# Four columns a chunk copied by TensorE through PSUM, in a graph layer's gather

## The chip, the cores and the metric

The kernel runs on one core of a Trainium2 chip. The metric is the time of one execution in device microseconds; the time before is the median of three runs. PE is TensorE, DVE is VectorE, ACT is ScalarE, POOL is GpSimd and SP is the engine that here issues most DMAs.

## The reference

One message-passing layer on a graph with 12,500 nodes of 48 numbers and 400,000 edges that are sorted by their target:

```python
h = jnp.maximum(_layernorm(x, axis=-1), 0.0)
x_i, x_j = h[dst], h[src]
tmp = jnp.concatenate([x_i, x_j, edge_attr], axis=1)   # 48 + 48 + 32
hid = jax.nn.relu(tmp @ W1 + b1)                       # 128 wide
out = jax.ops.segment_sum(hid @ W2 + b2, dst, num_segments=12500)
return x + out
```

All numbers are float32.

## The kernel before

`tmp @ W1` is split into three parts. A first stage (`node_tables`) makes two tables over the nodes, `tab_a` for the target's part with the bias and `tab_b` for the source's part, each with 128 numbers a node, in DRAM. Of `tab_b` it also keeps a copy in SBUF, turned round: `bt` has the 128 numbers on the partitions and the nodes along the free dimension.

The second stage (`windows`) goes over the edges in 391 chunks of 1024, each of 8 tiles of 128 edges. Targets are sorted, so a chunk's targets lie in a window of at most 80 nodes, and their part comes by a product: `prepare` has DVE compare the targets with the window's numbers (`lhs`, L437), and `before` multiplies that with the window's rows of `tab_a` and the edges' 32 numbers into the PSUM tile `pre` (L459). The sources are random. Their part is added to `pre` in `gathered` (L480), and a tile of 128 edges gets it in one of three ways:

- by a **gather** on POOL (L429): an indirect DMA fetches 128 rows of `tab_b` into `gb`, and a product with the identity adds them;
- by **columns** (L379): for each edge one instruction on DVE or ACT copies a column of `bt`, at an address from a register, into a column of a tile `gt`; a transposing product adds it. DVE fills 226 such tiles in the run and ACT 252;
- by **rows** (L335): SP issues a small DMA for each edge, 16 a chunk, into `gs`; 96 tiles.

Then `hidden` (L497, DVE) applies the relu and writes `hid`; `compare` (L448, DVE) makes the matrix `hot` that says to which node of the window each edge goes, from the numbers 0 to 79 in the PSUM tile `wnum`; `fold` (L507, L510) multiplies both into `p_g`, and `add` (L522, DVE) adds that to a running segment in SBUF. W2 is applied to whole segments.

The order is written out by hand in the loop at the end of `windows`, and each engine runs its own instructions in that order. In iteration c, PE does `before` and `gathered` of chunk c-1 and `fold` of chunk c-2. DVE does L437 of chunk c, columns (28), L497 of chunk c-2, columns (28), L448 of chunk c-1, columns (11), L522 of chunk c-3, columns (8). ACT does little but its 84 columns. The columns' numbers lie in `cols`, with `STRIP` numbers a chunk; `parts_of` cuts them into parts, and before each part the engine loads the part's numbers into registers (L318). `taken_by(c)` is the chunk that uses a tile which is filled in iteration c, 6 later and less toward the end. `STOP` is the iteration from which no more columns are copied. The tiles `gt` come from 13 buffers in turn, `gb` from 8 and 3, `pre` and `p_g` from two each.

Of the kernel before, what the change touches and what calls it, by code (L numbers as in the profile page):

```python
# [8 lines left out]
F32 = mybir.dt.float32  # L9
# [7 lines left out]
P = 128  # L17
N, D, DE, HID, E = 12500, 48, 32, 128, 400000
# [7 lines left out]
W = 80  # L26
# [29 lines left out]
END = NT // T  # L56


STRIP = 160
PLACE = 67  # L60
FEWER = 372
STOP = END - 3


def parts_of(c):

    dve = ((0, 20), (20, 8), (28, 20), (48, 8), (56, PLACE - 56), (68, 8))
    act = tuple((76 + 12 * k, 8 if k == 6 and c % 8 == 7 else 12) for k in range(7))
    return [(True, *of) for of in dve] + [(False, *of) for of in act]


def taken_by(c):

    lead = LEAD - max(0, c - FEWER + 1) * (LEAD - END + STOP) // (STOP - FEWER)
    return c + lead
# [3 lines left out]
BASE = 2 * RPART  # L79

BT0 = 16512
SEG0 = 144352
SEG_SIZE = 8 * L


# [9 lines left out]
def tiles_of(first, part):  # L95

    n = (END - 1 - first) * part // P
    return [first + (P * (j + 1) + part - 1) // part for j in range(n)]


AT = {}
COLS_OF = {}
for dve in (True, False):
    AT[dve] = [0]
    for c in range(STOP):
        AT[dve].append(AT[dve][-1] + sum(n for of, _, n in parts_of(c) if of == dve))
        for j in range(AT[dve][-2] // P, AT[dve][-1] // P):
            COLS_OF.setdefault(taken_by(c), []).append((dve, j))
BYROWS = tiles_of(ROWS0, RPART)
EPS = 1e-5  # L110

# [156 lines left out]
def windows(nc, tc, gp, bt, ident, idx, raw, rhss, x_t, tab_a, tab_b, dst, edge_t, w2s, b2s,  # L268
# [5 lines left out]
    with ExitStack() as es:  # L274
# [10 lines left out]
        gtc = es.enter_context(tc.tile_pool(name="gtc", bufs=GTS))  # L285
# [6 lines left out]
        ps_w = es.enter_context(tc.tile_pool(name="ps_w", bufs=1, space=PSUM))  # L292


        wnum = ps_w.tile([P, W], F32, name="wnum")
        nc.vector.tensor_copy(wnum, wrow)


        bt8 = bt.bitcast(U8)
# [3 lines left out]
        gts = {}  # L303
# [23 lines left out]
        def rows(c, nodes):  # L327

            for k, n in enumerate(nodes):
                e = (c - ROWS0) * RPART + k  # L330
                of = BYROWS[e // P]
                if of not in gss:
                    gss[of] = gtp.tile([P, HID], F32, name="gs")
                n = n.with_bounds(min_val=0, max_val=4 * HID * (N - 1))
                nc.sync.dma_start(  # L335
                    gss[of].bitcast(U8)[e % P : e % P + 1, :],
                    tab8[bass.ds(n, 4 * HID)].rearrange("(o h) -> o h", o=1),
                )
# [15 lines left out]
        def columns(c, part):  # L354

            parts = parts_of(c)
            dve, at, n = parts[part]
            place = PLACE if at < PLACE <= at + n and c >= LAG else None
            end = AT[dve][STOP] // P * P
            first = AT[dve][c] + sum(n for of, _, n in parts[:part] if of == dve) if c < STOP else end  # L360
            n = max(0, min(n, end - first))
            engine = mybir.EngineType.DVE if dve else mybir.EngineType.Activation
            copy = nc.vector.tensor_copy if dve else nc.scalar.copy
            size = -(-n // 4) * 4 if place is None else place + 1 - at
            if not n:
                if place is not None:
                    st[c - LAG]["base"], = numbers(c, place, 1, engine, cols)
                return
            got = numbers(c, at, size, engine, cols)
            if place is not None:  # L370
                st[c - LAG]["base"] = got[place - at]
            for k, to in enumerate(got[:n]):
                j, e = divmod(first + k, P)
                if (dve, j) not in gts:
                    gts[dve, j] = gtc.tile([HID, P], F32, name="gt")
                to = to.with_bounds(
                    min_val=BT0, max_val=BT0 + 4 * (NPAD - 1), guaranteed_mod_val=0, out_of_modulus=4
                ) - BT0
                copy(gts[dve, j][:, e : e + 1], bt8[:, bass.ds(to, 4)].bitcast(F32))  # L379

        def span(c):

            return next(w for w, last in SPANS if c < last)
# [59 lines left out]
        def compare(c):  # L443

            n, w = st[c]["n"], span(c)
            hot = wh.tile([P, T * W], F32, name="hot")
            hot = hot[:, : T * w].rearrange("p (t w) -> p t w", w=w)
            nc.vector.tensor_tensor(  # L448
                hot[:, :n, :], wnum[:, :w].unsqueeze(1).to_broadcast([P, n, w]),
                rel[:, c * T : c * T + n].unsqueeze(2).to_broadcast([P, n, w]), op=ALU.is_equal,  # L450
            )
            st[c]["hot"] = hot

        def before(c):

            s = st[c]
            pre = ps_p.tile([P, T, HID], F32, name="pre")
            for t in range(s["n"]):
                nc.tensor.matmul(  # L459
                    pre[:, t, :], s["lhs"][:K, t * P : (t + 1) * P], s["rhs"][:K, :],  # L460
                    start=t % BANK == 0, stop=False, skip_group_check=True,
                )
            s["pre"] = pre
# [49 lines left out]
        def add(c):  # L513

            s, w = st.pop(c), span(c)
            k = group(c)[0] % 2
            of = SEG0 + k * SEG_SIZE
            at = s["base"].with_bounds(
# [44 lines left out]
        def ending():  # L563
# [36 lines left out]
        with tc.manual_schedule():  # L600
            for c in range(NCH):
                a = c - LAG
                g, k = group(a)
                if c < RAW:
                    raw_turn(c)
                if c == 0:
                    columns(c, 0)
                    columns(c, 1)
                if c < NCH:
                    prepare(c)  # L610
                    rows(c, st[c].pop("rows"))
                if 0 <= c - 1 < NCH:
                    before(c - 1)
                    gathered(c - 1)
                if c:
                    columns(c, 0)
                    columns(c, 1)
                columns(c, 6)
                columns(c, 7)
                if 0 <= c - 2 < NCH:  # L620
                    hidden(c - 2)
                    fold(c - 2)
                columns(c, 2)
                columns(c, 3)
                columns(c, 8)
                columns(c, 9)
                if 0 <= c - 1 < NCH:
                    compare(c - 1)
                segment_add()
                columns(c, 4)  # L630
                if a >= 0:
                    add(a)
                    if a + 1 == begin(g + 1) < NCH:
                        segment_next(g)
                columns(c, 5)
                columns(c, 10)
                columns(c, 11)
                columns(c, 12)
                if c < 2:
                    nc.vector.memset(segs[c], 0.0)  # L640
                if a + 3 == begin(g + 1) < NCH or c == NCH - 1:
                    segment_load(g)
                if g > 0 and k < L // BLK:
                    segment_sum(g - 1, k, BLK)
                if g > 0 and k == (STORE if begin(g + 1) < NCH else 2):
                    segment_store(g - 1, L)
                if c == 1:
# [132 lines left out]
def tile_gnn_preln(  # L780
# [284 lines left out]
```

## Time and profile before

| | |
|---|---|
| median of 3 runs | 5453.94 us (5451.19 to 5468.6) |
| the profiled execution | 5457.1 us |
| its span, first to last instruction | 5455.4 us |
| mean granted TensorE clock | 0.688 |
| gathers on POOL (L429) | 2551, 944 ns each |
| bytes moved by DMA | 304.34 MB, mean 56 GB/s |

A profile is one execution. A row of a group reads: line, engine, operation, tile written and tile read, shape, count; then busy time and the mean in ns of one; then the time that the engine stood idle just ahead of such instructions, and what ended most of it. "Issue" means that nothing the profile shows ended the wait. A row of the list of waits reads: engine, tile and line, what it waited for, and then us in total, times, and the longest. A row of the timeline reads: start and length in us, engine, line, operation and count, with the idle time ahead of it in brackets. A row of windows reads: the stretch, its length, busy time with the number of instructions in parentheses, granted clock, DMA share, GB/s. Instructions that load registers or only wait are not counted as busy.

### The profile page before, as it was taken

How to read it: one execution, taken by the hardware profiler on the slowest of the kernel's cores; microseconds unless marked ns; L12 is line 12 of the kernel's file. 1: busy time of each engine (PE TensorE's matmuls, PEld its weight loads, DVE VectorE, ACT ScalarE, POOL GpSimd, SP SyncE). 2: the span in 40 equal slices, each digit the busy share in tenths (PEclk: the TensorE clock that was granted, in tenths of full speed). 3: DMA queues.
4: the chain of work that ended last, by engine and by line, in shares of the span. 5: the costliest groups of instructions: out<-in, count | busy, mean ns of one | idle time of the engine just before them, and what ended most of it. 6: DMA issues, size and time to landing. Idle time of an engine off the chain costs nothing.

```text
span 5455.4 us, 119545 instructions
## 1 busy us (share of the span) xinstructions
PE 3461.6 (63%) x15545; PEld 2861.3 (52%) x15545; DVE 3429.6 (63%) x31063; ACT 3389.1 (62%) x32359; POOL 2455.9 (45%) x2615
## 2 busy tenths in 40 slices
PE   4476666666566666666665656767565666665657
PEld 3365555555555555555555545555454555554546
DVE  4466666666666666666666666666666666666666
ACT  3366666666666666666666666666666665666664
POOL 4344444444444444444444444444444444444441
PEclk7566666666676666666677676666766666777678
DMA  3211111111111111111111111122211121222221
GB/s 123 89 49 46 48 47 48 47 47 49 50 52 48 51 51 52 51 52 51 54 56 53 56 52 54 56 57 56 58 56 56 56 58 54 59 63 61 62 61 42
DMA packets 148917, 304.34 MB, mean 56 GB/s; under 512 B 61811, under 2 KB 87685, under 8 KB 140325
## 3 DMA queue, kind: packets, MB, share of 16 engines
q0 software_dynamic: 83168, 168.53, 11.0%
q1 hardware_dynamic: 64530, 127.90, 7.8%
q14 instruction: 685, 5.61, 0.3%
q8 instruction: 130, 2.13, 0.2%
q10 hardware_dynamic: 404, 0.17, 0.0%
HBM read 280.57 MB, written 18.39 MB: 55 GB/s over the span
## 4 chain that ended last, share of the span: by engine, by line
DVE 57%; issue 33%; DVEq 4%; PE 3%; another core or an unknown queue 2%; DMA 0%; ACT 0%; SPq 0%; POOL 0%; ACTq 0%
DVE gt L379 36%; DVE lhs L437 8%; DVE hid L497 8%; DVEq L318 4%; DVE hot L448 3%; DVE seg L522 1%; PE p_g L507 1%; PE pre L459 1%; PE p_n L212 1%; PE pre L480 0%; DVE xseg L557 0%; DVE seg L538 0%; DMA gs<-tab_b 0%; ACT tab L221 0%
## 5 line engine op out<-in xcount | busy, mean ns | idle before, releaser
L379 ACT COPY gt<-bt 128x1 f32 x32256 | 3337.6, 187 | 1850.0 <-issue 1802.1
L429 POOL DMA_INDIRECT gb<-tab_b,srci x2551 | 2408.4, 944 | 2882.9 <-PE pre L480 1899.2
L379 DVE COPY gt<-bt 128x1 f32 x28928 | 2183.2, 145 | 1729.8 <-issue 1672.5
L507 PE MATMUL p_g<-hot,hid 128*128 128x64 f32 (+4 forms) x6250 | 1173.5, 356 | 1838.2 <-remote 878.3
L507 PEld LDWEIGHTS p_g<-hot,hid 128*128 128x128 f32 x6250 | 1127.3, 278 | 2038.8 <-remote 927.3
L459 PE MATMUL pre<-rhs,lhs 112*128 112x128 f32 x6250 | 1283.0, 388 | 1.4 <-DVE lhs L437 1.4
L459 PEld LDWEIGHTS pre<-rhs,lhs 112*128 112x128 f32 x6250 | 1188.8, 292 | 59.2 <-issue 36.3
L480 PE MATMUL pre<-gb,ident 128*128 128x512 f32 (+3 forms) x1540 | 752.3, 618 | 0.0
L497 DVE TENSOR_SCALAR hid<-pre 128x1024 f32<-128x1024 f32 x391 | 475.0, 1215 | 44.1 <-issue 33.8
L437 DVE TENSOR_SCALAR_CACHE_REDUCE lhs<-row,bw 64x1024 f32<-64x1024 int16 (+4 forms) x391 | 492.3, 1259 | 8.1 <-issue 6.8
L480 PEld LDWEIGHTS pre<-gb,ident 128*128 128x128 f32 x1540 | 342.9, 248 | 254.8 <-issue 252.8
L448 DVE TENSOR_TENSOR hot<-wnum,rel 128x512 f32<-128x512 f32 (+4 forms) x391 | 208.1, 532 | 76.5 <-issue 74.3
L480 PE MATMUL pre<-ident,gt 128*128 128x128 f32 x478 | 141.8, 355 | 0.0
L510 PE MATMUL p_g<-ident,deg 64*128 64x64 f32 (+4 forms) x391 | 119.0, 304 | 0.0
L522 DVE TENSOR_TENSOR seg<-seg,p_g 128x128 f32 (+4 forms) x390 | 93.7, 240 | 14.8 <-issue 9.9
L480 PEld LDWEIGHTS pre<-ident,gt 128*128 128x128 f32 x478 | 89.9, 195 | 0.0
L510 PEld LDWEIGHTS p_g<-ident,deg 64*128 64x128 f32 (+4 forms) x391 | 69.7, 178 | 23.7
L221 ACT COPY tab<-p_n 128x512 f32<-128x512 f32 (+1 forms) x37 | 18.8, 526 | 99.1 <-remote 71.8
L212 PE MATMUL p_n<-wa,ht 97*128 97x256 f32 x98 | 33.2, 497 | 51.9 <-DVE tab L219 30.8
L212 PE MATMUL p_n<-wb,ht 96*128 96x256 f32 x98 | 29.2, 452 | 42.8 <-ACT tab L221 35.8
L212 PEld LDWEIGHTS p_n<-wa,ht 97*128 97x128 f32 x98 | 22.6, 243 | 61.9 <-DVE tab L219 33.4
L219 DVE COPY tab<-p_n 128x512 f32<-128x512 f32 x17 | 11.5, 687 | 65.2 <-remote 40.9
(90 smaller groups left out, 462.2 us busy)
## 6 DMA issues: line engine op xcount, KB each, us to landing
gs<-tab_b SPq DMA_DIRECT2D x6144, 0.5 KB
lhs<-in_edge_t SPq DMA_DIRECT2D x195, 256.0 KB
gb<-tab_b,srci POOLq DMA_INDIRECT x2551
row<-in_dst SPq DMA_DIRECT2D x45, 256.0 KB
row<-in_dst SPq DMA_DIRECT2D x43, 192.0 KB
row<-in_dst SPq DMA_DIRECT2D x25, 320.0 KB
row<-in_dst SPq DMA_DIRECT2D x43, 128.0 KB
tab_b<-tab SPq DMA_DIRECT2D x4, 1152.0 KB
```

Of the source, the lines that this page charges most:

```text
L212: nc.tensor.matmul(p_n[:, q, :], ht[:rows, r0 // 2 + g + q, :], wt.rearrange("k a h -> k (a h)"), start=True, stop=True,)
L318: return nc.values_load_multi_w_load_instructions(table[c % P : c % P + 1, c // P, at : at + n], engines=[engine], min_val=0, max_val=1 << 23,
L379: copy(gts[dve, j][:, e : e + 1], bt8[:, bass.ds(to, 4)].bitcast(F32))
L429: nc.gpsimd.indirect_dma_start(out=gb[:, t, :], out_offset=None, in_=tab_b[:, :], in_offset=bass.IndirectOffsetOnAxis(ap=srci[:, c * T + t ...
L437: nc.vector.tensor_scalar(lhs[:w, : n * P], row[:w, : n * P], bw[:w, c : c + 1], None, op0=ALU.is_equal, op1=ALU.add, accum_out=deg[:w, :1],)
L448: nc.vector.tensor_tensor(hot[:, :n, :], wnum[:, :w].unsqueeze(1).to_broadcast([P, n, w]), rel[:, c * T : c * T + n].unsqueeze(2).to_broad ...
L459: nc.tensor.matmul(pre[:, t, :], s["lhs"][:K, t * P : (t + 1) * P], s["rhs"][:K, :], start=t % BANK == 0, stop=False, skip_group_check=True,)
L480: nc.tensor.matmul(pre[:, t:e, :].rearrange("p t h -> p (t h)"), lhsT, rhs, start=False, stop=True, is_transpose=turned, skip_group_check= ...
L497: nc.vector.tensor_scalar(h[:, :n, :], s["pre"][:, :n, :], 0.0, None, op0=ALU.max)
L507: nc.tensor.matmul(p_g[:, 0, :], s["h"][:, t, :], s["hot"][:, t, :], start=t == 0, stop=t == n - 1)
L510: nc.tensor.transpose(p_g[:, 1, :], s["deg"][:w, :], ident[:w, :w])
L522: nc.vector.tensor_add(to, to, s["p_g"])
```

## The change

A third engine copies columns. `parts_of` gets a 14th part of four columns for PE, so a chunk has 164 numbers in place of 160. For each of the four, PE multiplies the identity with the column of `bt`, which puts the column into a PSUM tile of 128 columns, one of two (`turned_of`). When 128 are there, after 32 iterations, `held_tile` has DVE copy the tile to a `gt` in SBUF, from where it is used like the others. No bank of PSUM was free for that: `wnum`, which DVE reads in L448, and `turned_of` are now parts of one tile, `held`, of one bank. `STOP` goes from 387 to 386.

```diff
-STRIP = 160
+STRIP = 164
-STOP = END - 3
+STOP = END - 4
...
+    pe = ((160, STRIP - 160),)
+    return [(by, *of) for by, all_of in ((DVE, dve), (ACT, act), (PE, pe)) for of in all_of]
...
-        wnum = ps_w.tile([P, W], F32, name="wnum")
+        held = ps_w.tile([P, 4, P], F32, name="held")
+        wnum, turned_of = held[:, 0, :W], held[:, 1:3, :]
...
+                of = bt8[:, bass.ds(to, 4)].bitcast(F32)
+                if by == PE:
+                    nc.tensor.matmul(
+                        turned_of[:, j % 2, e : e + 1], ident, of, start=True, stop=True,
+                        skip_group_check=True,
+                    )
+                    continue
...
+        def held_tile(c):
+
+            for j in range(AT[PE][c] // P, AT[PE][c + 1] // P) if 0 <= c < STOP else ():
+                gts[PE, j] = gtc.tile([HID, P], F32, name="gt")
+                nc.vector.tensor_copy(gts[PE, j], turned_of[:, j % 2, :])
...
                     rows(c, st[c].pop("rows"))
+                columns(c, 13)
                 if 0 <= c - 1 < NCH:
                     before(c - 1)
                     gathered(c - 1)
...
                     compare(c - 1)
+                held_tile(c - 1)
                 segment_add()
```

On PE, early in the second stage, one iteration stood like this before (`p_g` is written by the fold of chunk c-2, `pre` by `before` and `gathered` of the chunk after the next):

```order
L510 MATMUL p_g<-ident,deg_97 128x16
L459 MATMUL pre<-rhs_87,lhs_859 128x128 [waits DMAHW6_49,PE_49]
L459 MATMUL pre<-rhs_87,lhs_859 128x128 x7
L480 MATMUL pre<-ident,gt 128x128
L480 MATMUL pre<-gs,ident 128x128 [waits DMAHW4_49,DMAHW3_49,DMAHW5_49,DMAHW2_49,DMAHW7_49,DMAHW1_49,DMAHW0_49]
L480 MATMUL pre<-gb,ident 128x512 [waits DMASW2_49,DMASW7_49,DMASW1_49,DMASW0_49]
L480 MATMUL pre<-gb,ident 128x256 [waits DMASW4_49,DMASW3_49]
L507 MATMUL p_g<-hot,hid 128x16 [waits DVE_49]
```

And the same place now, where the lines are some 20 higher (L530 was L510, L479 was L459, L500 was L480, L527 was L507):

```order
L530 MATMUL p_g<-ident,deg_97 128x16
L323 TENSOR_LOAD cols
L385 MATMUL held<-bt,ident 128x1 [waits DVE_49]
L385 MATMUL held<-bt,ident 128x1 x3
L479 MATMUL pre<-rhs_87,lhs_859 128x128 [waits DMAHW6_49,PE_49]
L479 MATMUL pre<-rhs_87,lhs_859 128x128 x7
L500 MATMUL pre<-ident,gt 128x128
L500 MATMUL pre<-gb,ident 128x512 [waits DMASW2_49,DMASW7_49,DMASW1_49,DMASW0_49]
L500 MATMUL pre<-gb,ident 128x384 [waits DMASW5_49,DMASW4_49,DMASW3_49]
L527 MATMUL p_g<-hot,hid 128x16 [waits DVE_49]
```

Between the fold of one chunk and L479 there are now a load of registers and four products, and the first product waits for DVE: for the L468 (was L448) of the iteration before, which reads the same tile `held`.

On DVE, one piece of an iteration before, from the compare to the next chunk's L437 (`seg` is the running segment):

```order
L448 TENSOR_TENSOR hot<-wnum,rel 128x256 [waits PE_49]
L318 TENSOR_LOAD cols
L379 COPY gt<-bt 128x1 x11
L522 TENSOR_TENSOR seg_850<-seg_850,p_g 128x2x32 [waits DVE_49,PE_49]
L318 TENSOR_LOAD cols
L379 COPY gt<-bt 128x1 x8
L437 TENSOR_SCALAR lhs_858,deg_95<-row,bw 32x1024 [waits DMAHW4_49]
```

And now:

```order
L468 TENSOR_TENSOR hot<-held,rel 128x256 [waits PE_49]
L323 TENSOR_LOAD cols
L393 COPY gt<-bt 128x1 x11
L542 TENSOR_TENSOR seg_850<-seg_850,p_g 128x2x32 [waits DVE_49]
L323 TENSOR_LOAD cols
L393 COPY gt<-bt 128x1 x8
L457 TENSOR_SCALAR lhs_859,deg_101<-row,bw 32x1024
```

The copies are the same. The compare now waits for the products of its own iteration, which stand behind the fold on PE, and so the add that follows no longer needs a wait for that fold: it waits for DVE alone.

More of the change, by code (lines that the diff above doesn't have):

```diff
@@ L56 @@
 END = NT // T
-STRIP = 160
+STRIP = 164
 PLACE = 67
 FEWER = 372
-STOP = END - 3
+STOP = END - 4
+DVE, ACT, PE = "DVE", "ACT", "PE"
 def parts_of(c):
@@ L68, in parts_of @@
     act = tuple((76 + 12 * k, 8 if k == 6 and c % 8 == 7 else 12) for k in range(7))
-    return [(True, *of) for of in dve] + [(False, *of) for of in act]
+    pe = ((160, STRIP - 160),)
+    return [(by, *of) for by, all_of in ((DVE, dve), (ACT, act), (PE, pe)) for of in all_of]
 def taken_by(c):
@@ L81 @@
 BT0 = 16512
-SEG0 = 144352
+SEG0 = 144416
 SEG_SIZE = 8 * L
@@ L102 @@
 COLS_OF = {}
-for dve in (True, False):
-    AT[dve] = [0]
+for by in (DVE, ACT, PE):
+    AT[by] = [0]
     for c in range(STOP):
-        AT[dve].append(AT[dve][-1] + sum(n for of, _, n in parts_of(c) if of == dve))
-        for j in range(AT[dve][-2] // P, AT[dve][-1] // P):
-            COLS_OF.setdefault(taken_by(c), []).append((dve, j))
+        AT[by].append(AT[by][-1] + sum(n for of, _, n in parts_of(c) if of == by))
+        for j in range(AT[by][-2] // P, AT[by][-1] // P):
+            COLS_OF.setdefault(taken_by(c), []).append((by, j))
 BYROWS = tiles_of(ROWS0, RPART)
@@ L356, in columns @@
             parts = parts_of(c)
-            dve, at, n = parts[part]
+            by, at, n = parts[part]
             place = PLACE if at < PLACE <= at + n and c >= LAG else None
-            end = AT[dve][STOP] // P * P
-            first = AT[dve][c] + sum(n for of, _, n in parts[:part] if of == dve) if c < STOP else end
+            end = AT[by][STOP] // P * P
+            first = AT[by][c] + sum(n for of, _, n in parts[:part] if of == by) if c < STOP else end
             n = max(0, min(n, end - first))
-            engine = mybir.EngineType.DVE if dve else mybir.EngineType.Activation
-            copy = nc.vector.tensor_copy if dve else nc.scalar.copy
+            engine = {
+                DVE: mybir.EngineType.DVE, ACT: mybir.EngineType.Activation, PE: mybir.EngineType.PE
+            }[by]
             size = -(-n // 4) * 4 if place is None else place + 1 - at
@@ L373, in columns @@
                 j, e = divmod(first + k, P)
-                if (dve, j) not in gts:
-                    gts[dve, j] = gtc.tile([HID, P], F32, name="gt")
                 to = to.with_bounds(
@@ L378, in columns @@
                 ) - BT0
-                copy(gts[dve, j][:, e : e + 1], bt8[:, bass.ds(to, 4)].bitcast(F32))
+                of = bt8[:, bass.ds(to, 4)].bitcast(F32)
[5 more added lines that the diff above has]
+                    continue
+                if (by, j) not in gts:
+                    gts[by, j] = gtc.tile([HID, P], F32, name="gt")
+                copy = nc.vector.tensor_copy if by == DVE else nc.scalar.copy
+                copy(gts[by, j][:, e : e + 1], of)
+        def held_tile(c):
+            for j in range(AT[PE][c] // P, AT[PE][c + 1] // P) if 0 <= c < STOP else ():
+                gts[PE, j] = gtc.tile([HID, P], F32, name="gt")
+                nc.vector.tensor_copy(gts[PE, j], turned_of[:, j % 2, :])
         def span(c):
@@ L1010 @@
     strip = np.zeros((SLOTS * P, STRIP), np.int32)
-    for dve in (True, False):
+    for by in (DVE, ACT, PE):
         tiles = {
             j: c * T + T - len(js) + k
-            for c, js in COLS_OF.items() for k, (of, j) in enumerate(js) if of == dve
+            for c, js in COLS_OF.items() for k, (of, j) in enumerate(js) if of == by
         }
@@ L1018 @@
         for c in range(STOP):
-            slot = [at + k for of, at, n in parts_of(c) if of == dve for k in range(n)]
-            strip[c, slot] = nodes[AT[dve][c] : AT[dve][c + 1]]
+            slot = [at + k for of, at, n in parts_of(c) if of == by for k in range(n)]
+            strip[c, slot] = nodes[AT[by][c] : AT[by][c + 1]]
     strip[LAG : NCH + LAG, PLACE] = first
```

## The prediction

> **What bounds the kernel now.** I read the page first: busy shares, then the chain of waits that ended last.
>
> ```profile
> PE 3461.6 (63%) x15545; PEld 2861.3 (52%) x15545; DVE 3429.6 (63%) x31063; ACT 3389.1 (62%) x32359; POOL 2455.9 (45%) x2615
> ...
> DVE 57%; issue 33%; DVEq 4%; PE 3%; another core or an unknown queue 2%; DMA 0%; ACT 0%; SPq 0%; POOL 0%; ACTq 0%
> ```
>
> No engine is busy two thirds of the time, yet the chain is DVE's almost alone: 57% in its instructions, 33% in "issue" (it stands still and the profile shows nothing it waits for), 4% in its queue. So the second view is what the engines wait for, with the groups of the column copies and of L507 ahead of it.
>
> ```profile
> L379 ACT COPY gt<-bt 128x1 f32 x32256 | 3337.6, 187 | 1850.0 <-issue 1802.1
> ...
> L379 DVE COPY gt<-bt 128x1 f32 x28928 | 2183.2, 145 | 1729.8 <-issue 1672.5
> L507 PE MATMUL p_g<-hot,hid 128*128 128x64 f32 (+4 forms) x6250 | 1173.5, 356 | 1838.2 <-remote 878.3
> ...
> POOL gb L429 <- PE pre L480: 1899.2, 271, 64.4
> ACT gt L379 <- issue: 1802.1, 2898, 1.9
> DVE gt L379 <- issue: 1672.5, 2806, 1.9
> ...
> DVE hid L497 <- PE pre L480: 10.2, 5, 4.3
> ```
>
> DVE waits 10.2 us for PE's largest result in the whole run, so PE does not hold it up. PE idles 1838.2 us ahead of L507, which is 4.7 us in each of 391 iterations: that is PE's slack. POOL is not short either, since it waits 1899.2 us for PE to give buffers back. What remains is DVE's own 75 copies an iteration and the "issue" time in which ACT stands still as well, for nearly as long (1802.1 and 1672.5 us).
>
> That time belongs to the gathers. The third view, windows over one source line, counts iterations (L437 shows two instructions in each) and then gathers (L429):
>
> ```profile
> 1000.00:5000.00 4000.00, 372.47 (x588) 0.69 0.19 54
> 5360.20:5395.50 35.30, 5.10 (x8) 0.89 0.15 43
> 5265.70:5283.00 17.30, 1.28 (x2) 0.70 0.22 57
> ...
> 1000.00:5000.00 4000.00, 1842.04 (x1951) 0.69 0.19 54
> 5360.20:5395.50 35.30, 0.00 (x0) 0.89 0.15 43
> 5265.70:5283.00 17.30, 10.15 (x11) 0.70 0.22 57
> ```
>
> From 1000 to 5000 us, 294 iterations take 13.61 us each with 6.64 gathers each. Four iterations without a gather take 8.83 us each. One with 11 gathers takes 17.3. So an iteration is about 8.8 us of DVE's own work plus 0.72 us a gather (4.78 / 6.64), or 0.77 by the single one (8.47 / 11), though no buffer of that gather is waited for.
>
> **The change, part by part.** The sum is made against the profiled execution, 5457.1 us; the median of the three runs, 5453.94, is 3.2 us below it.
>
> *Eleven gathers fewer.* PE fills 12 tiles (1544 columns / 128) and ACT one less (251 for 252); DVE keeps 226. That leaves 2540 gathers for 2551. At 0.72 to 0.77 us each that is 7.9 to 8.5 us; the lower end is 0.66 (1672.5 / 2551), or 7.3. I take **-8 us**. A later start of POOL's bursts costs nothing: it has 1899.2 us of waiting in hand.
>
> *Columns end sooner.* DVE's last 53 copies (28928 - 75 x 385) fall into iteration 385 before and after, so nothing is saved there. ACT ends in iteration 384 for 386. These rows show the end:
>
> ```profile
> 5390.70 2.33 ACT L379 COPY gt<-bt 128x1 f32 x24 [0.18 <-issue]
> ...
> 5396.85 0.28 DVE L379 COPY gt<-bt 128x1 f32 x3
> ```
>
> ACT's last copies end at 5393.03 while DVE is still copying, so ACT's 128 copies fewer are worth **0**. If ACT set the pace they would be worth 20.6 us ((3337.6 + 1850.0) / 32256 x 128).
>
> *DVE's add has one wait less.* The order shows L522 with waits for DVE and PE before, and for DVE alone after. The second wait takes an instruction of its own in DVE's queue, one that only waits; in the two built programs these are 681 and 323 on DVE, 358 fewer. The profile does not count them, so their price is bounded by what stands around L522 in an iteration without gathers:
>
> ```profile
> 5361.65 1.89 DVE L379 COPY gt<-bt 128x1 f32 x28
> 5363.46 1.21 DVE L497 TENSOR_SCALAR hid<-pre 128x1024 f32<-128x1024 f32 x1
> 5364.74 1.89 DVE L379 COPY gt<-bt 128x1 f32 x28
> 5366.55 0.81 DVE L448 TENSOR_TENSOR hot<-wnum,rel 128x640 f32<-128x640 f32 x1
> 5367.30 0.76 DVE L379 COPY gt<-bt 128x1 f32 x11
> 5367.98 0.31 DVE L522 TENSOR_TENSOR seg<-seg,p_g 128x160 f32 x1
> 5368.43 0.58 DVE L379 COPY gt<-bt 128x1 f32 x8
> ...
> 5372.42 1.22 DVE L497 TENSOR_SCALAR hid<-pre 128x1024 f32<-128x1024 f32 x1
> ...
> 5375.53 0.81 DVE L448 TENSOR_TENSOR hot<-wnum,rel 128x640 f32<-128x640 f32 x1
> ```
>
> L522 ends at 5368.29 and the next copy starts at 5368.43: 0.14 us in which DVE computes nothing and only its queue (the wait, L522, the load of the next eight numbers) can be at work. So the wait costs between 0, if the load hides it, and 0.14 us. The nearest row is the copies' own cadence, 0.06 us an instruction (11 in 0.76, the last one 0.15 long). I take a little under that, 0.048 us: 358 x 0.048 = **-17 us**; the ends are 0 and -50. This is the largest term, and the change does not mean it.
>
> *Twelve copies from PSUM on DVE.* Nearest row: the add of one 128x128 tile out of PSUM.
>
> ```profile
> L522 DVE TENSOR_TENSOR seg<-seg,p_g 128x128 f32 x90 | 25.0, 277 | 0.6 <-issue 0.6
> ```
>
> 12 x 0.277 is 3.3 us; a copy's cadence alone, 0.06, gives 0.7. I take **+3 us**. The wait for PE in front of it is for products of the iteration before.
>
> *PE's load and four products.* L507 issues two matmuls for one of the source (6250 for 3125), so four products are eight pairs. Their pace is read from L507 fast and slow:
>
> ```profile
> 5272.26 3.70 PE L507 MATMUL p_g<-hot,hid 128*128 128x80 f32 x16 [6.63 <-DVE hid L497]
> ...
> 5289.55 3.70 PE L507 MATMUL p_g<-hot,hid 128*128 128x80 f32 x16 [8.43 <-DVE hid L497]
> ...
> 5361.96 1.88 PE L480 MATMUL pre<-gb,ident 128*128 128x512 f32 x4
> 5364.73 2.01 PE L507 MATMUL p_g<-hot,hid 128*128 128x80 f32 x16 [0.89 <-DVE hid L497]
> 5366.57 0.23 PE L510 MATMUL p_g<-ident,deg 80*128 80x80 f32 x1
> 5366.65 1.99 PE L459 MATMUL pre<-rhs,lhs 112*128 112x128 f32 x16
> 5368.47 0.38 PE L480 MATMUL pre<-ident,gt 128*128 128x128 f32 x2
> 5368.69 1.45 PE L480 MATMUL pre<-gb,ident 128*128 128x512 f32 x4
> 5373.69 2.65 PE L507 MATMUL p_g<-hot,hid 128*128 128x80 f32 x16 [3.54 <-DVE hid L497]
> ```
>
> Eight pairs are 1.0 us at the pace of 2.01 for 16, and 1.85 at that of 3.70. The load of four numbers stands behind L507's work and should pass under it; if not, it adds some tenths. The first product also waits for DVE's L448 of the iteration before, since both use the tile `held`. Behind it stand L459 and L480, and for these waits DVE's L497 an iteration later; POOL and SP wait for them too, with the slack named above. In the rows: L448 ends at 5367.36, 0.6 us after PE's fold; with 1.0 us of products L459 starts near 5368.4 for 5366.65, and L480 ends near 5371.9 for 5370.14. PE's next L507 starts at 5373.69, so 1.8 us of its 3.54 us gap stay. DVE has more cover still: the L480 that ends at 5363.84 is read by the L497 of 5372.42, 8.6 us later, and L448 comes back after 9.0 us. Where PE idles only 0.89 us it falls behind by about a microsecond and catches up next time. I put down **+4 us** for the tightest places; the ends are 0 and the rivals below.
>
> *Weighing one rule.* After 8.43 us of idling L507 ran at 3.70 us, after 0.89 at 2.01. The Trainium skill, "TensorE: Matmul & The Clock Gate", section "HAM oscillation — how this bites in real kernels", says that a gap of over about 3.4 us puts the array back to half its clock; the trace agrees here, 8.43 against 0.89. The rule speaks against the change, since the new wait cuts PE's work in two and makes a second gap. By it PE would need the slow pace more often, which is the third rival.
>
> Sum: -8 - 17 + 3 + 4 = -18; 5457.1 - 18 = 5439, and by the 3.2 us between profile and median, **5436 us**.
>
> **Rivals.**
> 1. *The second wait was hidden.* If the load of the next numbers starts no sooner, -17 goes: -8 + 3 + 4 = -1, about 5453. For it: the queue runs ahead of the engine. Against it: 0.14 us without work at that place. Chance 0.25.
> 2. *PE becomes the bound, slower than before.* Place: the load and four products at register-given addresses, behind L507. ACT's and DVE's copies, which have such addresses too, stood still 0.62 and 0.60 us at a time while gathers ran (1802.1 / 2898, 1672.5 / 2806). Eight matmuls held like that cost 4.8 us, with the 0.8 of a load like it 5.6. It decides above 4.7 us an iteration, PE's slack: 0.9 us over, 385 times, is +350 us, near 5790. Below that it bites only in runs without gathers, like the four iterations from 5360.2: PE's slow pass (3.70 for L507, as much for L459, 1.9 for L480, about 9 us as they overlap) with 3.7 us of products exceeds 8.8 by 3.9. Three such runs give 12 x 3.9 = 47 less a cover of 8.6 in each, +21 on the forecast, 5457. Against it: PE's own L507 of 5272.26 lies among 11 gathers and is no slower than that of 5289.55. Chance 0.10, half of it over the point.
> 3. *PE at the slow pace throughout.* About 9 us a pass and 1.85 of products are under 11: less than 13.6, so nothing where gathers run, and 2 us too much in an iteration without, of which the cover takes four in a run. With a few longer runs about +8 us on the forecast, 5444. Chance 0.07.
>
> **How the numbers follow.** The forecast has 0.58, with its own range 5422 to 5448 (the wait between 0.02 and 0.09 us). A measurement of this kernel tells about 0.3%, 16 us, from no change, so faster means under 5437.6. Of the forecast's 0.58 some 0.39 lie there; with a little of rival 3 that makes faster 0.40. Slower means above 5470: 0.12, most of rival 2 and mishaps of its kind. The rest, 0.48, is the same. The range, 5415 to 5463, takes in the first and third rival and the wait's price up to 0.11 us; it leaves out rival 2 above its point and the far end of the wait.
>
> **What would show it.** Gathers: 2540, with "issue" time at ACT's and DVE's copies some 8 us lower and no new waiting. The add's wait: the empty time behind L522 shrinks from 0.14 toward 0.09 us in iterations without gathers, and those shrink from 8.8 by about 0.05. PE: the products show 1 to 2 us an iteration, L507's idle time falls from 1838 toward 1000, and DVE's waits for PE stay below 20 us in all. I am wrong if DVE's L448 or L497 shows PE as releaser for more than that, if the products take over 4 us, or if the quick iterations get longer.

## The result, and the profile after

The changed kernel took 5521.95 us (median of four runs, 5511.57 to 5531.04), the kernel before 5456.47 us beside it: ratio 1.0116, 95% interval 1.0088 to 1.0145. The forecast was 5436 us, 18 us less; it came out 65 us more.

The experiments ran in five measurements, A to E, each on one chip with the kernel before beside it, and that kernel took 5454, 3538, 3536, 5457 and 5376 us. In B and C the "issue" time that the prediction begins with was hardly there in any kernel that was profiled. So every number below stands with its measurement, and ratios are taken within one.

The page of the profile after (columns as before; L393 was L379, L449 was L429, L527 was L507, L385 are PE's products, L399 DVE's copies of its tiles):

```profile
DVE 47%; issue 34%; ACT 11%; DVEq 3%; another core or an unknown queue 2%; ACTq 1%; PE 1%; SPq 0%; DMA 0%
...
L393 ACT COPY gt<-bt 128x1 f32 x32128 | 3349.2, 187 | 1954.2 <-issue 1935.2
L449 POOL DMA_INDIRECT gb<-tab_b,srci x2540 | 2396.7, 944 | 2964.7 <-PE pre L500 1893.9
L393 DVE COPY gt<-bt 128x1 f32 x28928 | 2190.8, 145 | 1782.2 <-issue 1726.7
L527 PE MATMUL p_g<-hot,hid 128*128 128x64 f32 (+4 forms) x6250 | 986.0, 319 | 869.7 <-DVE hid L517 540.8
```

ACT stands in the chain now, with 11%, and there are 11 gathers fewer, yet the "issue" time ahead of the column copies has grown: at ACT from 1802.1 to 1935.2 us, at DVE from 1672.5 to 1726.7. The list of waits tells whether each pause is longer or there are more of them (us in total, times, longest):

```profile
ACT gt L393 <- issue: 1935.2, 3095, 1.4
...
DVE gt L393 <- issue: 1726.7, 2891, 1.9
...
DVE hot L468 <- issue: 97.3, 127, 1.3
DVE hid L517 <- PE pre L500: 14.5, 5, 5.3
DVE hot L468 <- PE p_g L527: 4.6, 6, 2.1
```

There are more: 3095 for 2898 at ACT, 2891 for 2806 at DVE. One pause is as long as it was (0.625 us for 0.622 at ACT). DVE's waits for PE stay tiny, 14.5 and 4.6 us.

The windows over L457 (two instructions an iteration) and over L449 (one a gather), as the prediction read them:

```profile
1000.00:5000.00 4000.00, 369.59 (x582) 0.69 0.19 53
...
1000.00:5000.00 4000.00, 1809.56 (x1918) 0.69 0.19 53
```

291 iterations take 13.75 us each, with 6.59 gathers each. One without gathers takes 8.71 us by these rows of DVE's timeline, from one L457 to the next:

```profile
4030.97 1.26 DVE L457 TENSOR_SCALAR_CACHE_REDUCE lhs<-row,bw 64x1024 f32<-64x1024 int16 x1
...
4039.68 1.27 DVE L457 TENSOR_SCALAR_CACHE_REDUCE lhs<-row,bw 64x1024 f32<-64x1024 int16 x1
```

So a gather now costs (13.75 - 8.71) / 6.59 = 0.76 us, for 0.72 before. 2540 x 0.764 less 2551 x 0.720 is +104 us; the iteration's own work, 8.71 for 8.83, gives back 391 x 0.12 = 47. That is +57 of the 72 us between the two spans (5527.4 and 5455.4). The split is rough, since the two are not of one kind: the four iterations of before have windows of 80 nodes, and this one has 64 and one instruction more (L577 of 0.67 us, which was L557). One of its own kind before took 8.95 us:

```profile
3977.43 1.26 DVE L437 TENSOR_SCALAR_CACHE_REDUCE lhs<-row,bw 64x1024 f32<-64x1024 int16 x1
...
3986.38 1.26 DVE L437 TENSOR_SCALAR_CACHE_REDUCE lhs<-row,bw 64x1024 f32<-64x1024 int16 x1
```

Against that the work fell by more, and the price of a gather rose by more, with nearly the same sum. So the work got shorter, as forecast, and the standing still got longer; by how much each is not exact.

How a pause looks is seen in the timeline of the changed kernel, where POOL starts a burst of gathers at 3007.29 (start, length, and in brackets the idle time ahead of a row), first POOL, then ACT, then DVE:

```profile
3007.29 0.94 POOL L449 DMA_INDIRECT gb<-tab_b,srci  x1 [9.58 <-PE pre L500]
3008.54 0.94 POOL L449 DMA_INDIRECT gb<-tab_b,srci  x1 [0.30 <-issue]
```

```profile
2999.91 9.95 ACT L393 COPY gt<-bt 128x1 f32 x104
3010.14 0.28 ACT L393 COPY gt<-bt 128x1 f32 x2 [0.28 <-issue]
...
3012.32 0.19 ACT L393 COPY gt<-bt 128x1 f32 x1 [0.47 <-issue]
3013.03 0.19 ACT L393 COPY gt<-bt 128x1 f32 x1 [0.52 <-issue]
3013.75 0.19 ACT L393 COPY gt<-bt 128x1 f32 x1 [0.53 <-issue]
```

```profile
3012.33 0.15 DVE L393 COPY gt<-bt 128x1 f32 x1 [0.53 <-issue]
3013.04 0.15 DVE L393 COPY gt<-bt 128x1 f32 x1 [0.56 <-issue]
3013.76 0.15 DVE L393 COPY gt<-bt 128x1 f32 x1 [0.56 <-issue]
```

104 copies on end, and then one every 0.72 us, on both engines at the same moments (3012.32 and .33, 3013.03 and .04, 3013.75 and .76). And this is the same changed kernel in measurement C, while POOL starts a gather every 1.25 us (2000.08, 2001.33 and so on to 2006.33), the same pace as from 3007.29 above:

```profile
1999.83 3.92 ACT L393 COPY gt<-bt 128x1 f32 x40
2003.96 1.98 ACT L393 COPY gt<-bt 128x1 f32 x20 [0.21 <-issue]
```

```profile
ACT gt L393 <- PE pre L500: 192.5, 48, 12.8
...
DVE gt L393 <- issue: 174.4, 623, 1.1
...
ACT gt L393 <- issue: 53.9, 234, 0.8
```

The second fence is its list of waits. Hardly any pauses are left: 53.9 us for 1935.2 at ACT. POOL's pace is not what differs.

### The profile page after: what moved, and what is told of

Its sections match the earlier page's. It is cut to its first block, busy times and chain, and to the rows that moved or that the text cites. A ratio compares the mean times of both kernels' runs of the same rounds, so it can differ in the third digit from the quotient of the medians.

```text
span 5527.4 us, 125615 instructions
## 1 busy us (share of the span) xinstructions
PE 3737.2 (68%) x18626; PEld 3172.2 (57%) x18626; DVE 3439.7 (62%) x31075; ACT 3401.3 (62%) x32231; POOL 2444.3 (44%) x2604
## 4 chain that ended last, share of the span: by engine, by line
DVE 47%; issue 34%; ACT 11%; DVEq 3%; another core or an unknown queue 2%; ACTq 1%; PE 1%; SPq 0%; DMA 0%
DVE gt L393 30%; ACT gt L393 11%; DVE lhs L457 7%; DVE hid L517 6%; DVEq L323 3%; DVE hot L468 2%; ACTq L323 1%; DVE seg L542 1%; PE p_n L216 1%; SPq L340 0%; DVE xseg L577 0%; DVE seg L558 0%; ACT tab L225 0%; SPq L323 0%
## 5 line engine op out<-in xcount | busy, mean ns | idle before, releaser
L393 ACT COPY gt<-bt 128x1 f32 x32128 | 3349.2, 187 | 1954.2 <-issue 1935.2
L449 POOL DMA_INDIRECT gb<-tab_b,srci x2540 | 2396.7, 944 | 2964.7 <-PE pre L500 1893.9
L393 DVE COPY gt<-bt 128x1 f32 x28928 | 2190.8, 145 | 1782.2 <-issue 1726.7
L527 PE MATMUL p_g<-hot,hid 128*128 128x64 f32 (+4 forms) x6250 | 986.0, 319 | 869.7 <-DVE hid L517 540.8
L527 PEld LDWEIGHTS p_g<-hot,hid 128*128 128x128 f32 x6250 | 969.4, 241 | 1023.1 <-DVE hid L517 619.7
L479 PE MATMUL pre<-rhs,lhs 112*128 112x128 f32 x6250 | 1244.2, 380 | 0.0
L479 PEld LDWEIGHTS pre<-rhs,lhs 112*128 112x128 f32 x6250 | 1164.8, 287 | 2.5 <-issue 2.5
L385 PE MATMUL held<-bt,ident 128*128 x3072 | 568.4, 306 | 731.6 <-remote 604.0
L385 PEld LDWEIGHTS held<-bt,ident 128*128 128x128 f32 x3072 | 537.5, 264 | 800.8 <-remote 628.4
L500 PE MATMUL pre<-gb,ident 128*128 128x512 f32 (+3 forms) x1538 | 750.8, 618 | 0.0
L457 DVE TENSOR_SCALAR_CACHE_REDUCE lhs<-row,bw 64x1024 f32<-64x1024 int16 (+4 forms) x391 | 492.4, 1259 | 13.5 <-issue 12.5
L517 DVE TENSOR_SCALAR hid<-pre 128x1024 f32<-128x1024 f32 x391 | 474.5, 1213 | 20.0 <-PE pre L500 14.5
L500 PEld LDWEIGHTS pre<-gb,ident 128*128 128x128 f32 x1538 | 339.9, 246 | 254.5 <-issue 246.0
L468 DVE TENSOR_TENSOR hot<-held,rel 128x512 f32<-128x512 f32 (+4 forms) x391 | 208.3, 533 | 101.9 <-issue 97.3
L500 PE MATMUL pre<-ident,gt 128*128 128x128 f32 x489 | 142.5, 350 | 22.4 <-ACT gt L393 16.4
L530 PE MATMUL p_g<-ident,deg 64*128 64x64 f32 (+4 forms) x391 | 111.3, 285 | 0.0
L500 PEld LDWEIGHTS pre<-ident,gt 128*128 128x128 f32 x489 | 91.2, 194 | 24.1 <-ACT gt L393 17.8
L530 PEld LDWEIGHTS p_g<-ident,deg 64*128 64x128 f32 (+4 forms) x391 | 64.7, 165 | 20.8
L570 PE MATMUL p_f<-seg,w2s 128*48 128x512 f32 x56 | 42.9, 859 | 26.4 <-remote 23.5
```

The source lines that it names most:

```text
L385: nc.tensor.matmul(turned_of[:, j % 2, e : e + 1], ident, of, start=True, stop=True, skip_group_check=True,)
L393: copy(gts[by, j][:, e : e + 1], of)
L449: nc.gpsimd.indirect_dma_start(out=gb[:, t, :], out_offset=None, in_=tab_b[:, :], in_offset=bass.IndirectOffsetOnAxis(ap=srci[:, c * T + t ...
L457: nc.vector.tensor_scalar(lhs[:w, : n * P], row[:w, : n * P], bw[:w, c : c + 1], None, op0=ALU.is_equal, op1=ALU.add, accum_out=deg[:w, :1],)
L468: nc.vector.tensor_tensor(hot[:, :n, :], wnum[:, :w].unsqueeze(1).to_broadcast([P, n, w]), rel[:, c * T : c * T + n].unsqueeze(2).to_broad ...
L479: nc.tensor.matmul(pre[:, t, :], s["lhs"][:K, t * P : (t + 1) * P], s["rhs"][:K, :], start=t % BANK == 0, stop=False, skip_group_check=True,)
```

## The experiments

All ratios are to the kernel before in the same measurement, with their 95% interval. "Pauses" is the number of ACT's "issue" waits ahead of column copies in that run's profile.

| kernel | measurement | before, us | this, us | ratio | pauses |
|---|---|---|---|---|---|
| products ahead of the fold | A | 5454.37 | 5506.87 | 1.0118 [1.0085, 1.0151] | 3077 |
| fixed columns | A | 5454.37 | 5517.73 | 1.0126 [1.0089, 1.0163] | 3053 |
| tiles apart | A | 5454.37 | 5469.07 | 1.0032 [1.0014, 1.0050] | 2919 |
| numbers in SBUF alone | A | 5454.37 | 5436.78 | 0.9980 [0.9963, 0.9997] | 2942 |
| shared tile, one product | B | 3538.15 | 3513.86 | 0.9934 [0.9918, 0.9951] | 221 |
| shared tile, one product | C | 3536.35 | 3514.19 | 0.9942 [0.9925, 0.9958] | 221 |
| shared tile, one product | E | 5375.78 | 5439.31 | 1.0129 [1.0098, 1.0160] | 2957 |
| shared tile, four products | D | 5456.65 | 5529.51 | 1.0126 [1.0096, 1.0156] | 3066 |
| four products, no wait | B | 3538.15 | 3542.30 | 1.0015 [1.0006, 1.0025] | 230 |
| four products, no wait | C | 3536.35 | 3539.27 | 1.0003 [0.9987, 1.0018] | 236 |
| four products, no wait | E | 5375.78 | 5400.38 | 1.0042 [1.0021, 1.0062] | 2844 |
| eight products, no wait | D | 5456.65 | 5541.10 | 1.0151 [1.0112, 1.0190] | 2996 |
| the change | C | 3536.35 | 3515.30 | 0.9946 [0.9930, 0.9963] | 234 |
| the change, ACT 80 columns | B | 3538.15 | 3514.75 | 0.9939 [0.9922, 0.9956] | 236 |
| the change, ACT 80 columns | E | 5375.78 | 5454.06 | 1.0150 [1.0123, 1.0178] | 3038 |
| the change, DVE 71 columns | B | 3538.15 | 3375.24 | 0.9545 [0.9527, 0.9563] | 219 |
| the change, DVE 71 columns | C | 3536.35 | 3374.79 | 0.9551 [0.9535, 0.9567] | 225 |
| the change, DVE 67 columns | D | 5456.65 | 5551.44 | 1.0170 [1.0138, 1.0203] | 3132 |

### Measurement A: the wait, the register load, the shared tile

Two theories came first. W: the products' wait for the compare holds PE's further work, and the gathers come in step with DVE. R: PE's load of registers, and products at addresses from them, take part in the standing still.

Products ahead of the fold, where the compare they wait for is long over:

```diff
-                columns(c, 13)
                 if 0 <= c - 1 < NCH:
                     before(c - 1)
                     gathered(c - 1)
+                columns(c, 13)
```

> The change, with PE's load and four products moved behind the products into pre (L459, L480 of before) and ahead of the fold, so that they wait for a compare that ended some 6 us earlier. Theory W (the wait for DVE's compare holds PE's products into pre back, gather buffers come free in step with DVE, and the gathers stall ACT and DVE for longer): back to 5435 to 5455, PE's idle time at held near 0, ACT's issue time back near 1800 us. Theory R (PE's register load and register-addressed products take part in the stalls and lengthen them): unchanged, 5510 to 5530.

Measured: 5506.87. The loss stays, so W falls in this form, though not cleanly. This order brings waits of its own: the compare now waits for products that stand behind PE's work into `pre` (31.8 us in all), POOL waits for them 157.7 us, and PE has 15% of the chain, for 1% in the change:

```profile
DVE 46%; issue 29%; PE 15%; another core or an unknown queue 6%; DVEq 3%; ACT 0%; DMA 0%; ACTq 0%; SPq 0%
```

PE copies columns at fixed addresses, with no load (its 12 tiles hold other columns than the edges need):

```diff
+            if by == PE:
+                for k in range(n):
+                    j, e = divmod(first + k, P)
+                    nc.tensor.matmul(turned_of[:, j % 2, e : e + 1], ident, bt[:, e : e + 1], ...)
+                return
```

> The change, but PE copies columns at fixed addresses and loads no numbers, so the 12 tiles of PE hold wrong columns; waits, products and tiles stay. Theory W: unchanged, 5510 to 5530. Theory R: 5435 to 5455, ACT's issue time back near 1800 us.

Measured: 5517.73, as slow as the change. R falls.

The tile `held` is PE's alone, and the compare reads its numbers from SBUF, so there is no wait between products and compare, and the add keeps its second wait:

```diff
-        wnum, turned_of = held[:, 0, :W], held[:, 1:3, :]
-        nc.vector.tensor_copy(wnum, wrow)
+        wnum, turned_of = wrow, held[:, 1:3, :]
```

> The change, but the compare reads the window's numbers from SBUF, so held is PE's alone and neither the products wait for the compare nor the compare for the products; the add has its second wait again. Theory W: 5445 to 5465 (no gain from the wait that went). Theory R: 5510 to 5540. The compare itself may take another time from SBUF; the next kernel shows that.

Its control is the kernel before with only the numbers moved (`wnum = wrow`):

> The kernel before, with the compare reading the window's numbers from SBUF: a control for the kernel ahead of it. Both theories: within 15 us of before, if the compare takes as long from SBUF (0.28 to 0.82 us by width).

Measured: 5469.07, 4 us above what W gave and far below R, and 5436.78, 17.6 us under the kernel before, a little outside the range (the interval, 0.9963 to 0.9997, is barely clear of no change). Without the shared tile 15 us of the change's loss are left, 32 if counted from the control; by this comparison the rest hangs on the sharing, which the next runs try alone. Why the numbers in SBUF help is open; the compare itself takes as long (534 ns on average for 532).

### The shared tile alone

The kernel before with the tile shared and one product (or four) that nobody reads, between the fold and L459. This gives the compare a wait for PE, takes the add's second wait away, and adds no tile, no load and no earlier end:

```diff
-        wnum = ps_w.tile([P, W], F32, name="wnum")
+        held = ps_w.tile([P, 4, P], F32, name="held")
+        wnum, spare = held[:, 0, :W], held[:, 1:3, :]
...
+                for q in range(1):
+                    e = (1 * c + q) % P
+                    nc.tensor.matmul(spare[:, 0, e : e + 1], ident, bt[:, e : e + 1], ...)
                 if 0 <= c - 1 < NCH:
                     before(c - 1)
```

> The kernel before with the change's shared tile and one product of PE an iteration into its unused part, from a fixed column; nobody reads the product, there are no tiles of PE's, 2551 gathers. So the compare waits for PE's product, the product for the compare of the iteration before, and the add has no wait for PE of its own, but PE hardly works more. Theory S (the shared tile's waits make about half of the change's loss): 5475 to 5500 us. Theory N (the loss is the number of PE's added instructions): 5445 to 5468.

> The kernel before with the shared tile and one product of PE an iteration from a fixed column that nobody reads. Where the kernel before takes about 5450 us: theory S (the shared tile's waits make the loss) 5475 to 5510; theory N (the number of PE's added instructions makes it) 5440 to 5468. Where it takes about 3540: 3510 to 3520 by both.

> The kernel before with the shared tile and one product of PE an iteration. Where the kernel before takes about 5450 us: theory N (the number of products) 5440 to 5468; theory S (the shared tile's waits) 5485 to 5535. Where it takes about 3540: 3515.

> The kernel before with the shared tile and four products of PE an iteration from fixed columns that nobody reads: no tiles of PE's, 2551 gathers. Where the kernel before takes about 5450 us: theory S (the shared tile's waits make most of the loss) 5485 to 5520; theory N (PE's added instructions make it by themselves) 5455 to 5485, as with apart tiles. Where it takes about 3540: 3510 to 3525 by both, so that load, copies and the earlier end are worth nothing.

Where nothing pauses, one product in the shared tile gains 24 and 22 us (B, C). Where there are pauses it loses 64 us (E), and four lose 73 (D), for the change's 65. So the sharing with one product already brings a loss as large as the change's, as S said, though the change itself was not timed in D or E. S's ranges were for a kernel before of 5450 us: the ratio of E, 1.0129, comes to 5520 there, inside, and the 5529.51 of D lies 10 us above its range. What gains is seen in C, in DVE's timeline around the add, first with the second wait (four products, no wait on the compare), then without:

```profile
2008.61 0.25 DVE L522 TENSOR_TENSOR seg<-seg,p_g 128x96 f32 x1
2009.06 0.58 DVE L379 COPY gt<-bt 128x1 f32 x8 [0.21 <-issue]
```

```profile
2006.30 0.25 DVE L523 TENSOR_TENSOR seg<-seg,p_g 128x96 f32 x1
2006.69 0.58 DVE L380 COPY gt<-bt 128x1 f32 x8
```

From the add's end to the next copy it is 0.20 us with the wait and 0.14 without. Counted from the traces, DVE has 418 instructions that only wait for a semaphore in the first kernel and 53 in the second: 365 x 0.06 = 22 us, what was measured. (Before and in the change they are 417 and 59, 358 fewer, as the prediction had it.) The Trainium skill, "Perfetto Trace Analysis", section "Identifying Dependency Chains", notes that an instruction that waits for several engines may have separate waiting instructions put ahead of it; the trace agrees, and 0.06 us is their price here.

### The products alone

The kernel before with the numbers in SBUF, and four (or eight) products into a bank of their own; nobody waits:

```diff
-        wnum = ps_w.tile([P, W], F32, name="wnum")
-        nc.vector.tensor_copy(wnum, wrow)
+        held = ps_w.tile([P, 4, P], F32, name="held")
+        wnum, spare = wrow, held[:, 1:3, :]
...
+                for q in range(4):
+                    e = (4 * c + q) % P
+                    nc.tensor.matmul(spare[:, 0, e : e + 1], ident, bt[:, e : e + 1], ...)
```

> The kernel with the window's numbers in SBUF (5437 us) with four products of PE an iteration from fixed columns into a bank of their own; nobody reads them, so there is no new wait, no tile of PE's and no copy out of PSUM. Theory S (waits): 5427 to 5447, and the 32 us between the two kernels with apart tiles come from the copies, the load and the earlier end. Theory N (PE's four products in themselves): 5460 to 5475.

> The window's numbers in SBUF and four products of PE an iteration from fixed columns into a bank of their own that nobody reads. Where the kernel before takes about 5450 us: theory S 5427 to 5450; theory N 5460 to 5480. Where it takes about 3540: 3535 to 3550 by both.

> The window's numbers in SBUF and four products of PE an iteration into a bank of their own, no wait. Where the kernel before takes about 5450 us: theory N (products cost by themselves) 5460 to 5485, between the kernel without (5437) and that with eight (5541); theory S (only waits cost, and eight products are another matter, PE as the bound) 5430 to 5450. Where it takes about 3540: 3540.

> The window's numbers in SBUF and eight products of PE an iteration into a bank of their own, with no wait. Where the kernel before takes about 5450 us: theory S 5427 to 5455; theory N 5480 to 5520 (twice the 32 us of the kernel with apart tiles). Where it takes about 3540: 3540 to 3560 if PE has slack left beside 92% busy time, 3600 and more if it becomes the bound (1.2 us an iteration).

Where nothing pauses, four products cost 4 and 3 us (the latter within the noise), though PE is busy 92% of the span. With pauses they cost 25 us (E; by its ratio 5473 where the kernel before takes 5450, inside N's range), and eight cost 84 (D, 21 us above N's range). All of it is counted from the kernel before; the numbers in SBUF by themselves were worth -17.6 us in A, so the products may cost more. So N is right as well: with pauses, products cost time without any new wait. The waits of the kernel with eight, in D:

```profile
POOL gb L429 <- PE pre L480: 2148.3, 353, 77.2
ACT gt L379 <- issue: 1877.1, 2996, 1.9
DVE gt L379 <- issue: 1730.7, 2759, 2.0
```

No wait of DVE's or ACT's for PE is among the longer ones (DVE's largest is 20.6 us), only POOL's, and the chain has PE at 3%, so PE has not become the bound. ACT has 2996 pauses, where the kernel before had 2898 in the first profile with the same gathers.

### Which engine sets the pace

The change with four columns fewer on ACT, or with four or eight fewer on DVE; POOL gathers 12 or 24 tiles more:

```diff
-    act = tuple((76 + 12 * k, 8 if k == 6 and c % 8 == 7 else 12) for k in range(7))
+    act = tuple((76 + 12 * k, 12 - 4 * (k == 6) - 4 * (k == 6 and c % 8 == 7)) for k in range(7))
```

```diff
-    dve = ((0, 20), (20, 8), (28, 20), (48, 8), (56, PLACE - 56), (68, 8))
+    dve = ((0, 20), (20, 8), (28, 20), (48, 4), (56, PLACE - 56), (68, 4))
```

This is the one with 67; the one with 71 has (48, 8) as before.

> The changed kernel with four of ACT's columns fewer in each iteration (80 for 84), which costs 12 gathers more. Theory A (since the change ACT's copies set the pace, and DVE follows through the tiles): 5440 to 5475, until DVE is next. Theory D (DVE sets the pace as before): 5515 to 5540, since only gathers are added.

> The changed kernel with four of ACT's columns fewer in each iteration (80 for 84), 12 gathers more. Where the kernel before takes about 5450 us: theory A (ACT sets the pace) 5400 to 5470, since 4 x 0.103 us x 385 are 159 us, until DVE is next, 9 us back for the gathers; theory G (the time is that of the gathers' standing still, whoever it hits) 5530 to 5545. Where it takes about 3540: 3515 as in the run before.

> The changed kernel with four of DVE's columns fewer in each iteration (71 for 75), which costs 12 gathers more. Theory A (ACT sets the pace): 5515 to 5545. Theory D (DVE sets the pace): 4 x 0.06 us an iteration without stalls are 92 us, less 9 for the gathers: 5430 to 5460. Between the two if both engines share one limit.

> The changed kernel with four of DVE's columns fewer in each iteration, which costs 12 gathers more. Where the kernel before takes about 5450 us: theory A (ACT sets the pace since the change) 5515 to 5545; theory D (DVE sets it) 5400 to 5450, since 4 x 0.09 us are 140 us where nothing stands still, less where it does. Where it takes about 3540: 3365 to 3385 by both.

> The changed kernel with eight of DVE's columns fewer in each iteration (67 for 75), 24 or 25 gathers more. Where the kernel before takes about 5450 us: theory A (ACT sets the pace since the change) 5525 to 5560; theory D (DVE sets it) 5380 to 5450. Where it takes about 3540: 3235 to 3300, the lower end if DVE stays the bound (8 x 0.091 us x 385), the upper if ACT or PE takes over.

And the change itself in C:

> The change as it is, beside the runs of the other kernels of this call. Where the kernel before takes about 5450 us (ACT and DVE stand still while gathers run): 5505 to 5535 by every theory. Where it takes about 3540 us (they do not): 3510 to 3530 if the add's lost wait is worth its 24 us there and the rest of the change adds a few; 3540 to 3560 if the change itself is what is slow.

Where nothing pauses, the answer is DVE: 1536 copies fewer (27,392 for 28,928) gain 140 us on the change (3374.79 for 3515.30), 0.091 us each, and ACT's are worth nothing. With pauses neither is worth anything. ACT with four fewer: 1.0150, no better than the 1.0116 of the change beside the result. That refutes A here, and by the ratio it is 5532 where the kernel before takes 5450, inside the range of theory G. DVE with eight fewer: 1.0170, and 5551.44 refutes D and lies in A's range. Two rows show why, the chain of the former (E; the profile follows it over some 70% of the span) and that of the latter (D):

```profile
DVE 43%; issue 23%; DVEq 3%; PE 1%; SPq 0%; DMA 0%
```

```profile
ACT 55%; issue 35%; ACTq 6%; PE 2%; DVE 1%; another core or an unknown queue 1%; DMA 0%; POOL 0%; DVEq 0%
```

The last column copies of each engine say the same, first with ACT relieved, then with DVE relieved:

```profile
5370.94 6.05 ACT L393 COPY gt<-bt 128x1 f32 x64 [0.46 <-issue]
...
5396.04 1.71 DVE L393 COPY gt<-bt 128x1 f32 x25
```

```profile
5479.52 0.63 DVE L393 COPY gt<-bt 128x1 f32 x9
...
5518.31 4.93 ACT L393 COPY gt<-bt 128x1 f32 x52 [0.19 <-issue]
```

Whichever engine is relieved, the other ends last, by 21 us and by 43: with the pauses in, both are about equally long. Theory A alone and theory D alone are both wrong; a gain there needs fewer pauses for both, or less work for both, which no run tried. That ACT had joined DVE could be read from the end of the first profile after:

```profile
5503.64 3.82 ACT L393 COPY gt<-bt 128x1 f32 x40 [0.19 <-issue]
```

```profile
5464.57 1.71 DVE L393 COPY gt<-bt 128x1 f32 x25
```

These are the last column copies of each. ACT ends at 5507.46, 41 us after DVE's 5466.28; before, it ended at 5393.03, ahead of DVE, whose last 25 copies began at 5400.22.

### What stays open

Why products and the shared tile bring more pauses is not settled. Counted over the profiled executions, one pause's length hardly moves (0.61 to 0.64 us at ACT), and the number a gather is 1.14 before, 1.15 with tiles apart, 1.15 with the numbers in SBUF, and 1.20 to 1.22 with the tile shared (3053, 3077 and 3095 for 2540). In E it is 1.16 with one product in the shared tile and 1.11 with four apart. ACT's count alone does not carry the whole time: with the numbers in SBUF it is 2942, more than before, and that kernel is the quicker one.

One reading is that POOL's bursts of gathers fall into step with DVE's iterations. Counted from the traces for iterations 20 to 374, with a burst beginning where POOL idled over 0.4 us, 344 of the 355 iterations of the change see exactly one burst begin, and 176 before. In E it is 335 with one product in the shared tile and 289 with four apart, and in A 273 with tiles apart: among these, the more in step, the slower. The new waits are not needed for it, since eight products with no wait reach 343. Against it, with the products ahead of the fold only 218 do, and the loss is nearly the same, though PE is in the chain there; and with 67 columns on DVE, where ACT ends last, 171 do. No run moved the bursts alone, so this is a reading and not shown. Nor did a run share the tile and keep the add's second wait, and the kernel before was profiled only beside the result, not in A to E.

Whether it is the chip or the hour that brings the pauses is open too. The record numbers the chips of A to E as 6, 5, 0, 7 and 0, so chip 0 had hardly any in C and had them in E; if that is one and the same chip, it is not the chip alone.

## Why the prediction was wrong

**The price of a gather** is the step that failed. The prediction put 11 gathers fewer at 0.72 to 0.77 us each, -8 us, and so took for granted that a change elsewhere leaves the number of pauses a gather alone; that "a later start of POOL's bursts costs nothing" is the same assumption. They went from 1.14 to 1.22 (ACT's, 2898 / 2551 and 3095 / 2540): +197 pauses and +133 us at ACT, +85 and +54 us at DVE, which run side by side and do not add up. "Issue" was to fall by 8 us. What made the pauses more frequent stays open; which edits do it is shown above.

**The new wait at +4 us** stood on DVE's waits for PE staying small. They did, and the sign named for it (below 20 us) held: 14.5 and 4.6. But the tile behind that wait, shared with one product, costs 64 us by itself where engines pause, sixteen times the term. The rows named for that step could not show its cost, since nobody waits for PE in them.

**The add's second wait at -17 us** was right: 22 and 24 us where nothing pauses, 0.06 us each for the 0.048 put down. Rival 1 (it was hidden) is refuted there. The sign named for it was read from one short gap: over all 369 adds that a copy follows, the median gap went from 0.20 us before to 0.14 in the change, not from 0.14 toward 0.09.

**The copies from PSUM at +3 us**: this row of the change gives 3.4.

```profile
L399 DVE COPY gt<-held 128x128 f32<-128x128 f32 x12 | 3.4, 284 | 0.4 <-issue 0.3
```

**ACT's earlier end at 0** rested on ACT being ahead of DVE, and that no longer held: ACT now ends last, by 41 us. No run shows the term alone. Together with the load, PE's tiles and 11 gathers fewer it makes no difference clear of the noise, since four products in the shared tile without them give 1.0126 for the change's 1.0116.

**The sum.** Where nothing pauses, the change is worth -21 us (3515.30 for 3536.35), and the sum was -18. That is where the argument holds, but not the case it was made for, and the agreement is partly luck: the add's lost wait makes all of it, and 11 gathers cost nothing there, since one product in the shared tile gives 3514 with 11 gathers more. The -8 has no counterpart in it.

**Rival 2**, the one slower case, had the wrong mechanism. PE's products took no 4.7 us:

```profile
L385 PE MATMUL held<-bt,ident 128*128 x3072 | 568.4, 306 | 731.6 <-remote 604.0
```

568.4 us over 384 iterations are 1.48 us each, within the forecast's 1 to 2, and PE still idles 869.7 + 731.6 us ahead of its two jobs. Rival 3, after the rule on the clock gate: L527 did not slow down with a second gap, it took 986.0 us for the 1173.5 of L507.

**The chances.** Slower had 0.12, all of it on PE as the bound and on mishaps. A term was missing for the resource that is already the second largest in the chain, 33% "issue": what lengthens or adds to it was never asked. Rival 2 did price the engines' standing still, but for PE's products alone, not for ACT and DVE.

## What to carry to other kernels

Where a profile shows a third of the chain as time that nothing explains, hold its price for a variable and not for a constant: ask of each edit whether it can change how often that time strikes, and give that a rival of its own. Relieve one of two engines that run side by side only if the other's own total, pauses included, is well below. And measure such a kernel in more than one place: sharing the tile with one product was worth -24 us in one and +64 in another.

## What the runs showed of the hardware

The kernel before took 5376 to 5457 us in four measurements, the one of the result among them, and 3536 to 3538 in two. The kernels that were profiled have column copies of the same length in all of them (187 ns on ACT); the difference is in the pauses while gathers run. The granted TensorE clock differed as well, 0.81 in the two quick ones for 0.69, and no run shows which of the two follows from the other. The pauses hit ACT and DVE at the same moments, and one instruction passes every 0.72 us. The Trainium skill, "SBUF — State Buffer", section "SBUF: two separate sides", states that a DMA cannot be slowed by a compute operation nor the reverse, and that ACT never waits for anyone's port; here each copy on ACT takes its 187 ns, but while gathers run the next one starts late, 1935.2 us in all. The rule speaks of ports; these pauses lie between instructions, so it gives no price for them, and the measurement decides.

Four products at addresses from registers, eight pairs of a weight load and a product, took 1.48 us with pauses and 1.24 without (477.3 us over 384 iterations, the row below, of the change in C), with PE busy 68% and 92% of the span.

```profile
L385 PE MATMUL held<-bt,ident 128*128 x3072 | 477.3, 276 | 54.2 <-DVE hot L468 43.4
```
